# Local attention on one Trainium2 core: probabilities as the stationary operand, v with a ones column as the moving one

## The chip, the cores and the metric

The kernel runs on one core of one Trainium2 chip. The metric is the device time of one execution in microseconds (us), lower being better. Before the change it is 3192.31 us, the median of three runs (3188.84 to 3196.97).

A core has a matrix engine (TensorE, "PE" in the profile, its weight loads listed as "PEld"), a vector engine (VectorE, "DVE"), a scalar engine (ScalarE, "ACT"), a general engine (GpSimd, "POOL") and a queue that issues transfers (SyncE, "SP"). Matrix products land in PSUM, eight banks of 512 float32 values on each of 128 partitions. Everything here is float32.

## The reference

The input is `x`, 8 sequences of 1024 tokens of 256 values. The program first adds a causal latent attention with 16 heads (not touched here), and then a two-layer local transformer. One layer of that is, cut to what matters:

```python
h = shift_token(x)
q, k, v = split(h @ wqkv, 3)            # 8 heads of 64
q, k = rotary_xpos(l2norm(q) * qs, l2norm(k) * ksc)
# windows of 128 queries; each sees its own window and the one before
sim  = einsum('bhwid,bhwjd->bhwij', bq * 8, bk)      # j over 256 keys
mask = (i < j) | (i > j + 128) | (j == -1)
attn = softmax(where(mask, -max, sim))
o    = einsum('bhwij,bhwjd->bhwid', attn, bv)
x = x + o @ wo
x = x + geglu_mlp(layernorm(shift_token(x)))
```

A query `i` of a window sees the keys `j <= i` of its own window and the keys `j >= i` (counted within the window) of the previous one. Of the 128 x 128 square of a query window with its own keys the lower triangle counts, of that with the previous window's keys the upper one.

## The kernel before

The first third of the time is the latent attention. The rest, `local`, works through 128 windows: 2 layers x 8 sequences x 8 windows of 128 tokens. A `Pass` is one layer of one sequence, hence 8 windows `i` = 0 to 7. One loop runs over steps (line 1277), and in each step several windows are at work, each at another stage, so that the engines always have something to do. The order of the instructions on PE, DVE, ACT and POOL is the order in which this loop writes them (`manual_schedule`); the order on SP is not written by hand. In step `s` the loop calls:

- `both` of window `s-4`, then `qk` of window `s` (the product for q and k, norms and rotation), `transposes` of window `s-1`, `v` of window `s`. `transposes` turns q and k in 32 x 32 squares on DVE and then sends them to DRAM and back, which puts the squares into place: four writes of 128 KB and a read of 512 KB on SP.
- an `output` that was put off (see below), a unit of the MLP if one is due, `values` of window `s-4`, and `scores` of window `s-3`.
- the rest of an MLP product if one is pending (`rests`), `divide` of window `s-4`, `output` for the pair of windows `s-6` and `s-5` when `s` is even, and another unit of the MLP. If an MLP product was pending in this step, `output` is put off to the next one (`held`).

`scores` (L999) computes keys x queries: k stationary, q moving, and for each key quarter of 32 only the 160 query columns that can count (fewer in window 7, which has no following window). ACT exponentiates, and POOL sets the masked entries to zero with two `affine_select` per group of four heads. So the probabilities `pts[i][g]` lie with the keys on the partitions; columns 0 to 127 are the queries of the same window, columns 128 to 255 those of the next.

`values` (L1044) makes `v` stationary, 32 columns at a time (L1057), and moves 128 columns of probabilities through it. The four heads of a group write the four 32-partition quarters of the PSUM tile `o`, so four matmuls run side by side. The output is transposed: head dimension on the partitions, queries in the columns, which is what `output` needs as stationary operand. The sums of the exponentials come from a further product with a stationary matrix of ones (L1065) over `both`, for which DVE adds the two squares of probabilities first (L1041). `divide` (L1070) takes the reciprocal of the sums over 128 x 256 values (L1075), multiplies (L1080), and keeps two control sums (L1079, L1084). `output` (L1088) multiplies by `wo` through `times` (L722), which splits the 128 stationary columns into four quarters.

`load_o` (L775) puts the rows of `wo` in the order in which `values` leaves the head dimensions on the partitions. The pools `pacc` (one bank) and `psum` (three banks, tag `mm`) hold `o` and the sums.

Of the kernel before, what the change touches and what calls it, by code (L numbers as in the profile page):

```python
# [29 lines left out]
F32 = mybir.dt.float32  # L30
# [23 lines left out]
LOW, HIGH = 1e-30, 1e10  # L54
# [4 lines left out]
DEPTH, HEADS, DH, WINDOW = 2, 8, 64, 128  # L59
INNER = HEADS * DH  # L60
# [23 lines left out]
def preln_mla_local_kernel(  # L84
# [627 lines left out]
    def local(ctx: ExitStack, verdict):  # L712
# [4 lines left out]
        p1 = ctx.enter_context(tc.tile_pool(name="l1", bufs=1))  # L717
        p2 = ctx.enter_context(tc.tile_pool(name="l2", bufs=2))

        QUARTER = [slice(32 * n, 32 * n + 32) for n in range(4)]  # L720

        def times(out, w, rhs, start, stop):  # L722
            for four in QUARTER:
                nc.tensor.matmul(out[four], w[:, four], rhs, start=start, stop=stop)  # L724

        ppair = [ctx.enter_context(tc.tile_pool(name="pair0", bufs=1, space=PSUM))]
        psum = ctx.enter_context(tc.tile_pool(name="psum3", bufs=3, space=PSUM))
        ppair.append(ctx.enter_context(tc.tile_pool(name="pair1", bufs=1, space=PSUM)))
        pacc = ctx.enter_context(tc.tile_pool(name="pacc3", bufs=1, space=PSUM))
        evac = Evacuate(nc, "a")  # L730

        ones = p1.tile([P, 32], F32, name="ones_l")
        nc.gpsimd.memset(ones, 1.0)
# [53 lines left out]
        def load_mlp(l):  # L787
# [126 lines left out]
        qkT = p1.tile([P, PLACES + 1, 4, 2, 4, 32], F32, name="qkT")  # L914
        zs = [dram.tile([P, 4, 2 * P], F32, tag=f"z{i}", name=f"z{i}") for i in range(4)]
        zxs = [dram.tile([P, 4, 2 * P], F32, tag=f"zx{i}", name=f"zx{i}") for i in range(2)]
        zhs = [dram.tile([P, 4, 2 * P], F32, tag=f"zh{i}", name=f"zh{i}") for i in range(2)]


# [5 lines left out]
        class Pass:  # L925
# [43 lines left out]
            def v(self, i):  # L969
                key = self.key(i)  # L970
                pv = psum.tile([P, INNER], F32, tag="mm", name=f"pv{key}")
                for c in range(2):
                    times(pv, self.left(i)[c], self.w["qkv"][:, c, 2 * INNER :], c == 0, c == 1)
                self.vs[i] = p1.tile([P, INNER], F32, tag="v", name=f"v{key}", bufs=6)
                evac(self.vs[i], pv)

            def transposes(self, i):

# [53 lines left out]
                        )  # L1032
                    self.pts[i].append(pt)

            def both(self, i):

                self.sums = [self.pts[i][g][:, :, :P] for g in range(2)]
                if i:
                    for g in range(2):
                        t = p1.tile([P, 4, P], F32, tag="both", name=f"both{self.key(i)}_{g}", bufs=2)  # L1040
                        nc.vector.tensor_tensor(t, self.sums[g], self.pts[i - 1][g][:, :, P:], ALU.add)  # L1041
                        self.sums[g] = t

            def values(self, i):  # L1044

                key, vs, pts = self.key(i), self.vs, self.pts
                blocks = [(i - 1, P)] if i else []
                blocks.append((i, 0))
                o = pacc.tile([P, 2, 2, P], F32, tag="acc", name=f"o{key}")
                s = psum.tile([P, 2, P], F32, tag="mm", name=f"s{key}")  # L1050
                place = lambda j: 2 * (j % 2) + j // 2
                for g in range(2):
                    for a in range(2):
                        for m, off in blocks:
                            for j in range(4):
                                h = 4 * g + j
                                nc.tensor.matmul(  # L1057
                                    o[32 * j : 32 * j + 32, g, a, :],
                                    vs[m][:, h * DH + a * 32 : h * DH + a * 32 + 32],
                                    pts[m][g][:, place(j), off : off + P],  # L1060
                                    start=(m == blocks[0][0]), stop=(m == i),
                                )
                for g in range(2):
                    for j in range(4):
                        nc.tensor.matmul(  # L1065
                            s[32 * j : 32 * j + 32, g, :], ones, self.sums[g][:, place(j), :], start=True, stop=True
                        )
                self.done[i] = o, s

            def divide(self, i):  # L1070

                key, vs, pts, oTs = self.key(i), self.vs, self.pts, self.oTs
                o, s = self.done.pop(i)
                rs = p1.tile([P, 2, P], F32, tag="lrs", name=f"rs{key}")
                nc.vector.reciprocal(rs, s)  # L1075
                if i % 2 == 0:
                    oTs[i // 2] = p2.tile([P, 4, 2 * P], F32, tag="oT", name=f"oT{key}")
                at = self.n * NT + i
                nc.vector.tensor_reduce(stats[:, 1, at : at + 1], s, AX.XY, ALU.add)  # L1079
                nc.vector.tensor_tensor(  # L1080
                    oTs[i // 2][:, :, (i % 2) * P : (i % 2 + 1) * P].rearrange("p (g a) q -> p g a q", g=2),
                    o, rs.unsqueeze(2).to_broadcast([P, 2, 2, P]), ALU.mult,
                )
                nc.vector.tensor_reduce(stats[:, 0, at : at + 1], rs, AX.XY, ALU.add)  # L1084
                if i:
                    del vs[i - 1], pts[i - 1]

            def output(self, n):  # L1088

                oT = self.oTs.pop(n)  # L1090
                x_, y, key = self.x_, self.y, f"{self.b}_{self.l}"
                two = slice(2 * n, 2 * n + 2)
                ps = psum.tile([P, 2, D], F32, tag="mm", name=f"psw{key}_{n}")
                for i in range(2):
                    for c in range(4):
                        times(ps[:, i, :], oT[:, c, i * P : (i + 1) * P], self.w["o"][:, c, :], c == 0, c == 3)
                nc.vector.tensor_tensor(x_[:, two], ps, x_[:, two], ALU.add)

                rows = slice(2 * n * P, (2 * n + 2) * P)
                nc.sync.dma_start(y[rows, :P].rearrange("(t p) d -> p t d", p=P), x_[:, two, :P])  # L1100
                rows = slice(2 * n * P + 1, (2 * n + 2) * P + 1)
                nc.sync.dma_start(y[rows, P:].rearrange("(t p) d -> p t d", p=P), x_[:, two, P:])
                m, o = divmod(2 * n + 2, ST)
                if o == 0:
                    self.hs[m - 1] = p2.tile([P, ST, D], F32, tag="h", name=f"h{key}_{m - 1}")
                    rows = slice((m - 1) * CH, m * CH)
                    nc.sync.dma_start(self.hs[m - 1], y[rows].rearrange("(t p) d -> p t d", p=P))
# [138 lines left out]
        windows = len(passes) * NT  # L1246
# [29 lines left out]
        with tc.manual_schedule(engines={E.PE, E.DVE, E.Activation, E.Pool}):  # L1276
            for step in range(windows + LAG):
                n, i = divmod(step, NT)
                if step < windows and i == 0:
                    l, b = passes[n]  # L1280
                    if n and b == 0:
                        o = w["o"]
                        w = load_attention(l)
                        w["o"] = o
                    made[n] = Pass(n, l, b, w, *ready.pop(n))
                late = step < windows and n and i == 0 and b == 0
                each(step, "both", 4)
# [5 lines left out]
                while held:  # L1293
                    j = held.pop()
# [33 lines left out]
            for _ in units:  # L1328
                while rests:
                    rests.pop()()  # L1330

        ok = p1.tile([P, 2, B * DEPTH * NT], F32, name="okl")
        for m, top in enumerate((HIGH, 1 / LOW)):
            nc.vector.tensor_scalar(ok[:, m, :], stats[:, m, :], top, None, ALU.is_le)
        verdict.add(ok.rearrange("p m n -> p (m n)"), "local")


    def general_mla(ctx: ExitStack):
# [513 lines left out]
    verdict = Verdict()  # L1852
# [93 lines left out]
```

## Time and profile before

| | |
|---|---|
| median of three runs | 3192.31 us |
| the profiled execution | 3190.63 us, with a span of 3188.9 us |
| granted PE clock in it, as a share | 0.993 |
| `local`, windows of attention and MLP | from about 915 us to the end |

The profile is of a single execution. "Span" is the time from its first to its last instruction. In a row of the costliest groups stand the line, the engine, the operation, what it writes and reads, the shapes and the count; behind the bar the busy time of the group, the mean nanoseconds of one instruction, and the idle time of the engine before it with what ended it. Every float32 matmul of the kernel stands in the trace as two PE records, and as many weight loads. The mean of one PE record is its latency, not what it costs: matmuls overlap, and a length for a whole batch is read from the chain of waits, which lists stretches of the critical path as start, length, engine, tile, line and number of records.

### The profile page before, as it was taken

What the parts mean: (1) busy time and instruction counts of PE and PEld (TensorE: products, weight loads), DVE (VectorE), ACT (ScalarE), POOL (GpSimd) and SP (SyncE); (2) the same over time, 40 slices, a digit from 0 to 9 for tenths busy, and PEclk for the clock granted to TensorE, in tenths of its full rate; (3) what the DMA queues carried; (4) which work ended last, traced back from release to release, by engine and by line L of the source; (5) the groups of instructions that cost most, each with busy time, mean ns of one, the idle gap of its engine ahead of it and who ended that gap; (6) DMA issues with size and microseconds to landing.
All of it is one profiled execution on the core that took longest, in us unless ns stands there. A gap on an engine that the chain in (4) does not pass through costs nothing.

```text
span 3188.9 us, 112507 instructions
## 1 busy us (share of the span) xinstructions
PE 3112.4 (98%) x49986; PEld 1447.9 (45%) x49986; DVE 2619.9 (82%) x3848; ACT 1705.4 (53%) x2114; POOL 1381.7 (43%) x1065
## 2 busy tenths in 40 slices
PE   7999999999878999999999999999999999999998
PEld 2344444444333444445554444454544445444453
DVE  5999999999879878788887878777777877778773
ACT  6888988898722444444444444444444444444441
POOL 1011111110057656565565655555555556555540
PEclk9999999999998999999999999999999999999999
DMA  5333434333334454454544445455545545454431
GB/s 138 76 100 95 104 92 108 96 99 87 108 114 120 106 132 117 125 131 117 135 116 132 116 126 157 124 144 141 144 118 136 132 124 134 137 144 121 121 105 56
DMA packets 411613, 376.98 MB, mean 118 GB/s; under 512 B 174655, under 2 KB 353262, under 8 KB 410990
## 3 DMA queue, kind: packets, MB, share of 16 engines
q1 hardware_dynamic: 409134, 367.29, 43.4%
q8 instruction: 394, 6.46, 0.8%
q10 hardware_dynamic: 1984, 2.41, 0.2%
q14 instruction: 101, 0.83, 0.1%
HBM read 173.82 MB, written 141.00 MB: 99 GB/s over the span
## 4 chain that ended last, share of the span: by engine, by line
PE 67%; DVE 2%; DMA 1%; SPq 1%; POOL 0%; issue 0%; ACT 0%; DVEq 0%; ACTq 0%; POOLq 0%
PE ag L724 19%; PE pair L724 13%; PE psy L724 10%; PE psw L724 7%; PE pv L724 6%; PE o L1057 6%; PE pair L1016 5%; PE s L1065 2%; DMA z<-turned 0%; SPq L904 0%; DMA qkT<-z 0%; DMA zx<-turneds 0%; DVE turned L984 0%; DVE rs L1075 0%; SPq L987 0%
## 5 line engine op out<-in xcount | busy, mean ns | idle before, releaser
L483 DVE TENSOR_TENSOR pt<-pt,er 128x1024 f32<-128x1024 f32 x576 | 676.3, 1220 | 31.9 <-ACT pt L469 26.9
L960 POOL TENSOR_TENSOR t<-t,t 128x1024 f32<-128x1024 f32 x128 | 304.3, 2377 | 803.0 <-DVE t L956 803.0
L724 PE MATMUL ag<-d,l 128*32 128x512 f32 x5632 | 639.7, 593 | 0.9 <-ACT d L1146 0.4
L469 ACT ACTIVATE pt<-sc 128x1024 f32<-128x1024 f32 x576 | 560.2, 1029 | 88.8 <-PE sc L461 72.4
L1022 ACT ACTIVATE pt<-pair 128x1024 f32<-128x1024 f32 (+1 forms) x256 | 235.5, 969 | 538.3 <-PE pair L1016 497.1
L724 PE MATMUL pair<-l_qkv,xT 128*32 128x512 f32 x4096 | 473.6, 598 | 4.1 <-DMA xT<-zx 2.6
L127 POOL TENSOR_TENSOR rn<-ss,half 128x16 f32<-128x16 f32 x128 | 373.0, 2914 | 13.9
L724 PEld LDWEIGHTS ag<-d,l 128*32 128x32 f32 x5632 | 178.5, 110 | 372.6 <-issue 351.6
L423 POOL TENSOR_SCALAR_AFFINE_SELECT er<-er 128x128 f32<-128x128 f32 x64 | 74.3, 1169 | 599.5 <-ACT er L421 598.7
L496 PE MATMUL acc<-pt,v 128*32 128x512 f32 (+3 forms) x3072 | 330.0, 498 | 3.8 <-DVE pt L483 3.5
L951 ACT ACTIVATE sq<-pair 128x1024 f32<-128x1024 f32 x128 | 131.3, 1026 | 348.9 <-issue 308.9
L724 PE MATMUL psy<-l,hid 128*32 128x256 f32 x5120 | 282.1, 379 | 0.0
L724 PEld LDWEIGHTS pair<-l_qkv,xT 128*32 128x32 f32 x4096 | 132.8, 111 | 305.0 <-issue 278.0
L461 PE MATMUL sc<-q,k 32*128 32x512 f32 (+3 forms) x3072 | 248.3, 380 | 13.2 <-DVE x L576 6.9
L953 DVE TENSOR_TENSOR t<-pair,l_cos 128x1024 f32<-128x1024 f32 x128 | 156.0, 1219 | 122.8 <-ACT sq L951 122.5
L966 POOL TENSOR_TENSOR t<-t,rn 128x1024 f32<-128x1024 f32 x128 | 243.5, 1902 | 10.0
L724 PE MATMUL pv<-l_qkv,xT 128*32 128x512 f32 x2048 | 247.1, 592 | 0.0
L1189 DVE SCALAR_TENSOR_TENSOR hid<-ag,l_b,ge 128x512 f32<-128x512 f32 x160 | 116.7, 730 | 158.5 <-ACT ge L1188 87.8
L1057 PEld LDWEIGHTS o<-pt,v 128*32 128x32 f32 x7680 | 215.4, 110 | 67.5 <-issue 51.3
L461 PEld LDWEIGHTS sc<-q,k 32*128 32x128 f32 x3072 | 140.3, 183 | 217.4 <-ACT pt L469 157.4
L1057 PE MATMUL o<-pt,v 128*32 128x128 f32 x7680 | 234.5, 273 | 3.1 <-POOL pt L1024 2.8
L1075 DVE RECIPROCAL rs<-s 128x256 f32<-128x256 f32 x128 | 223.1, 1743 | 15.8 <-PE s L1065 15.7
(266 smaller groups left out, 4532.9 us busy)
## 6 DMA issues: line engine op xcount, KB each, us to landing
z<-turned SPq DMA_DIRECT2D x512, 128.0 KB
qkT<-z SPq DMA_DIRECT2D x128, 512.0 KB
y<-xs SPq DMA_DIRECT2D x128, 128.0 KB
h<-y SPq DMA_DIRECT2D x32, 512.0 KB
zx<-turneds SPq DMA_DIRECT2D x120, 128.0 KB
xT<-zx SPq DMA_DIRECT2D x240, 64.0 KB
zh<-turnedh SPq DMA_DIRECT2D x120, 128.0 KB
d<-zh SPq DMA_DIRECT2D x30, 512.0 KB
```

The costliest lines, as they stand in the source:

```text
L127: nc.gpsimd.tensor_tensor(out_, in_, half[:, :n], ALU.pow)
L461: nc.tensor.matmul(two[n // 2][:, n % 2, lo : lo + w], k[rows], q[rows, h], start=(h == 1), stop=(h == 0),)
L469: nc.scalar.activation(pt, sc, AF.Exp, scale=SCALE)
L483: nc.vector.tensor_tensor(t, t, er.to_broadcast([P, 1024 // w, w]), ALU.mult)
L496: nc.tensor.matmul(self.acc[g][32 * n : 32 * n + 32, q0 - c * 512 :], self.v[:, kb, h * VW - at : h * VW - at + 32], pts[n // 2][:, n % 2, ...
L724: nc.tensor.matmul(out[four], w[:, four], rhs, start=start, stop=stop)
L960: nc.gpsimd.tensor_tensor(t1, t1, t2, ALU.add)
L966: nc.gpsimd.tensor_tensor(t1, t1, rn.unsqueeze(3).to_broadcast([P, 2, HEADS, DH]), ALU.mult)
L1016: nc.tensor.matmul(flat[keys, 2 * j + c, q0:q1].rearrange("p (b t) -> p b t", t=32), qkT[rows, at, t, 1, 2 * g + c, :], q[rows, q0 // 32 : ...
L1022: nc.scalar.activation(pt[:, :, : n * P], flat[:, :, : n * P], AF.Exp, scale=-1.0)
L1057: nc.tensor.matmul(o[32 * j : 32 * j + 32, g, a, :], vs[m][:, h * DH + a * 32 : h * DH + a * 32 + 32], pts[m][g][:, place(j), off : off + ...
L1075: nc.vector.reciprocal(rs, s)
```

## The change

`values` is turned around. The probabilities become the stationary operand, 32 queries at a time, and `v` of one head is the moving operand, with a column of ones behind its 64 columns, so 65 columns. The output then has the queries on the partitions, and column 64 of each head is the sum of its exponentials. `v` is kept in a ring of six tiles whose ones column is written once.

Of the two squares of each head, the parts that the mask leaves empty are partly left out. Queries 0 to 63 see only keys 0 to 63 of their own window, and queries 64 to 127 see only keys 64 to 127 of the previous one. So for each head and query quarter there are one matmul over all 128 keys and one over 64 keys. First come all the matmuls over 128 keys, then all those over 64; the column quarters and the two PSUM banks are arranged so that consecutive matmuls fall on different parts of the array. In window 0 of a pass, which has no previous window, one of the two matmuls falls away.

`divide` takes two small reciprocals, multiplies twice, and then transposes the 128 x 512 result in 32 x 32 squares on DVE. After every odd window the pair goes to DRAM in four transfers and comes back in one, as q and k do. `output` uses this as the stationary operand. `both`, the ones matrix, the product of sums and the two control sums fall away; the control sums are replaced by a check of the kept reciprocals every 32 windows. `wo` is loaded in its natural order with one transfer.

```diff
-        ones = p1.tile([P, 32], F32, name="ones_l")
-        stats = p1.tile([P, 2, B * DEPTH * NT], F32, name="stats")
+        LOOK = 32
+        stats = p1.tile([P, LOOK, 2, 4], F32, name="stats")
+        VL = DH + 1
+        vring = [p1.tile([P, HEADS, VL], F32, name=f"lv{i}") for i in range(6)]
+        for t in vring:
+            nc.gpsimd.memset(t[:, :, DH:], 1.0)
...
         def load_o(l):
-            for g in range(2):
-                for j in range(4):
-                    h = 4 * g + j
-                    nc.sync.dma_start(
-                        w[32 * j : 32 * j + 32, 2 * g : 2 * g + 2],
-                        wo[l, h * DH : (h + 1) * DH].rearrange("(a p) e -> p a e", a=2),
-                    )
+            nc.sync.dma_start(w, wo[l].rearrange("(c p) e -> p c e", p=P))
...
-                evac(self.vs[i], pv)
+                self.vs[i] = vring[(self.n * NT + i) % len(vring)]
+                evac(self.vs[i][:, :, :DH], pv.rearrange("p (h d) -> p h d", d=DH))
...
-            def both(self, i):
...
+            def values(self, i):
+                banks = [
+                    pool.tile([P, 512], F32, tag=tag, name=f"o{key}_{r}")
+                    for r, (pool, tag) in enumerate(((pacc, "acc"), (psum, "mm")))
+                ]
+                o = [t[:, : 4 * VL].rearrange("p (h d) -> p h d", d=VL) for t in banks]
+                place = lambda j: 2 * (j % 2) + j // 2
+                todo = []
+                for h in range(HEADS):
+                    todo += [(h, s, i - 1 if s < 2 else i, slice(0, P)) for s in range(4)]
+                for n in range(4):
+                    for r in range(2):
+                        h = 4 * (n // 2) + 2 * r + n % 2
+                        todo += [
+                            (h, s, *((i, slice(0, 64)) if s < 2 else (i - 1, slice(64, P)))) for s in range(4)
+                        ]
+                todo = [(h, s, m, rows, (h // 2 % 2, (s + h // 2 * 2) % 4)) for h, s, m, rows in todo if m >= 0]
+                first, last = ({at: n for n, (*_, at) in every} for every in (
+                    reversed(list(enumerate(todo))), enumerate(todo)
+                ))
+                for n, (h, s, m, rows, (r, c)) in enumerate(todo):
+                    g, j = divmod(h, 4)
+                    q0 = 32 * s + (P if m < i else 0)
+                    nc.tensor.matmul(
+                        o[r][32 * c : 32 * c + 32, 2 * g + h % 2, :], self.pts[m][g][rows, place(j), q0 : q0 + 32],
+                        self.vs[m][rows, h, :], start=first[r, c] == n, stop=last[r, c] == n,
+                    )
+                self.done[i] = o
+
+            def divide(self, i):
+                o = self.done.pop(i)
+                on = p1.tile([P, INNER], F32, tag="on", name=f"on{key}")
+                for r in range(2):
+                    rs = stats[:, (self.n * NT + i) % LOOK, r]
+                    nc.vector.reciprocal(rs, o[r][:, :, DH])
+                    nc.vector.tensor_tensor(
+                        on.rearrange("p (g r j d) -> p r g j d", g=2, r=2, j=2)[:, r],
+                        o[r][:, :, :DH].rearrange("p (g j) d -> p g j d", g=2),
+                        rs.rearrange("p (g j) -> p g j", g=2).unsqueeze(3).to_broadcast([P, 2, 2, DH]), ALU.mult,
+                    )
+                if i % 2 == 0:
+                    self.ot = p1.tile([P, 4, 2, 4, 32], F32, tag="ot", name=f"ot{key}")
+                nc.vector.transpose(self.ot[:, :, i % 2], on.rearrange("p (y x d) -> p x y d", y=4, x=4))
+                if i % 2:
+                    z = zos[i // 2 % 2]
+                    for c in range(4):
+                        nc.sync.dma_start(
+                            z.rearrange("(x p) c f -> p x c f", p=32)[:, :, c],
+                            self.ot[32 * c : 32 * c + 32].rearrange("p x i y t -> p x (i y t)"),
+                        )
+                    oTs[i // 2] = p2.tile([P, 4, 2, 4, 32], F32, tag="oT", name=f"oT{key}")
+                    nc.sync.dma_start(
+                        oTs[i // 2].rearrange("p c i y t -> p (c i y t)"), z.rearrange("p c f -> p (c f)")
+                    )
...
             def output(self, n):
-                        times(ps[:, i, :], oT[:, c, i * P : (i + 1) * P], self.w["o"][:, c, :], c == 0, c == 3)
+                        for s, four in enumerate(QUARTER):
+                            nc.tensor.matmul(
+                                ps[four, i, :], oT[:, (s + 2 * c) % 4, i, c, :], self.w["o"][:, c, :],
+                                start=c == 0, stop=c == 3,
+                            )
...
-                each(step, "both", 4)
...
+                if step >= 4 and (step - 3) % LOOK == 0 and step - 4 < windows:
+                    inverses = stats.rearrange("p n r h -> p (n r h)")
+                    ok = p1.tile([P, INNER], F32, tag="on", name=f"okl{step}")[:, : LOOK * HEADS]
+                    nc.vector.tensor_scalar(ok, inverses, 1 / LOW, None, ALU.is_le)
+                    nc.vector.scalar_tensor_tensor(ok, inverses, 1 / HIGH, ok, ALU.is_ge, ALU.mult)
+                    verdict.add(ok, "local")
```

More of the change, by code (lines that the diff above doesn't have):

```diff
@@ L730, in local @@
         evac = Evacuate(nc, "a")
-        ones = p1.tile([P, 32], F32, name="ones_l")
-        nc.gpsimd.memset(ones, 1.0)
         rest_hid = p1.tile([P, CH // 2], F32, name="rest_hid")
@@ L916, in local @@
         zxs = [dram.tile([P, 4, 2 * P], F32, tag=f"zx{i}", name=f"zx{i}") for i in range(2)]
+        zos = [dram.tile([P, 4, 2 * P], F32, tag=f"zo{i}", name=f"zo{i}") for i in range(2)]
         zhs = [dram.tile([P, 4, 2 * P], F32, tag=f"zh{i}", name=f"zh{i}") for i in range(2)]
@@ L973, in v @@
                     times(pv, self.left(i)[c], self.w["qkv"][:, c, 2 * INNER :], c == 0, c == 1)
-                self.vs[i] = p1.tile([P, INNER], F32, tag="v", name=f"v{key}", bufs=6)
-                evac(self.vs[i], pv)
+                self.vs[i] = vring[(self.n * NT + i) % len(vring)]
+                evac(self.vs[i][:, :, :DH], pv.rearrange("p (h d) -> p h d", d=DH))
             def transposes(self, i):
@@ L1033, in scores @@
                     self.pts[i].append(pt)
-            def both(self, i):
-                self.sums = [self.pts[i][g][:, :, :P] for g in range(2)]
-                if i:
[L1039 to L1086, printed above, removed]
+            def values(self, i):
+                key = self.key(i)
+                banks = [
[25 more added lines that the diff above has]
+                self.done[i] = o
@@ new lines, in divide @@
+            def divide(self, i):
+                key, oTs = self.key(i), self.oTs
+                o = self.done.pop(i)
[22 more added lines that the diff above has]
+                    )
+                if i:
+                    del self.vs[i - 1], self.pts[i - 1]
@@ L1330, in local @@
                     rests.pop()()
[L1332 to L1335, printed above, removed]
     def general_mla(ctx: ExitStack):
```

## The prediction

> **What bounds the kernel now.** I read the engine totals first, then the stretch in which the windows run steadily (1250 to 3100 us), then the chain of waits.
>
> ```profile
> PE 3112.4 (98%) x49986; PEld 1447.9 (45%) x49986; DVE 2619.9 (82%) x3848; ACT 1705.4 (53%) x2114; POOL 1381.7 (43%) x1065
> 1250.00:3100.00 1850.00, 1845.87 (x33132) 906.57 (x33128) 1472.67 (x2324) 807.55 (x956) 1036.87 (x767) 1.00 0.49 130
> ```
>
> The second line gives the busy time of PE, weight loads, DVE, ACT and POOL in these 1850 us, then the PE clock (full), the DMA share and GB/s. PE is idle for 4.1 us of 1850, DVE for 377. A busy PE need not be a fast one, so I ask whether its batches last as long as their columns take. Three rows by shape and seven pieces of the chain of waits:
>
> ```profile
> L1057 PE MATMUL o<-pt,v 128*32 128x128 f32 x7680 | 234.5, 273 | 3.1 <-POOL pt L1024 2.8 <-DVE oT L1080 0.2
> L1016 PE MATMUL pair<-qkT 64*32 64x160 f32 x7168 | 152.2, 304 | 19.2 <-DMA qkT<-z 16.0 <-DVE t L956 2.8 <-issue 0.5
> L1016 PE MATMUL pair<-qkT 64*32 64x32 f32 x256 | 14.3, 200 | 0.6 <-issue 0.6
> ...
> 2022.13 1.75 PE o L1057 x64
> 2023.87 0.44 PE s L1065 x16
> 2024.31 1.25 PE pair L1016 x64
> ...
> 2037.73 0.87 PE o L1057 x32
> ...
> 2040.29 3.59 PE psw L724 x64
> ...
> 2078.39 0.86 PE psy L724 x32
> ...
> 3109.42 1.04 PE pair L1016 x30
> ```
>
> From 160 to 32 columns a record gets 104 ns shorter, 0.81 ns a column; I use 0.833, with which the batches come out. Four records run side by side on the four column quarters: 64 records of 128 columns are 64 x 128 x 0.833 / 4 = 1.71 us, and the chain has 1.75, which is 0.7 ns more per record. With 64 rows, two halves of the rows work at once as well: the rest of psy, 32 records of 256 columns over eight parts, is 0.85 us by this sum and 0.86 in the chain. So PE time is columns moved, divided by the parts that work at once, and what shortens this stream shortens the kernel.
>
> **PE: the values.** Removed per window: 1.75 (L1057) + 0.44 (L1065) = 2.19 us; in the 16 first windows of a pass, 0.87 + 0.44 = 1.31.
>
> Added: 32 matmuls of 128 keys, 64 records of 65 columns over four parts: 64 x (65 x 0.833 / 4 + 0.7) = 0.91 us. Then 32 of 64 keys, 64 records over eight parts: 0.43 us by columns. Here records would start every 7 ns, and the question is whether PE can be fed so fast. The nearest row is the last piece above, the scores of window 7 (its list is short because the rest of psy starts among them; by line it has 64 records). Its longest column quarter, 128 columns, sets the stream at 0.85 us, and it takes 1.04, a record every 16 ns; the excess of 0.19 is that of the other scores (1.25 against 1.07). In the trace the first 16 records of a scores batch start within 133 ns, and later, where nothing was queued, new matmuls (two records each) come 16.7 ns apart. That feed, 8.35 ns a record, makes 0.53 us; with some matmuls queued from the slower part before, I take 0.50. Sum 1.41 us, 0.78 saved, x 112 = 87 us. Bounds: 0.43 without any limit at the feed, against 16 ns a record throughout, which gives 2.09 and saves 0.10.
>
> First windows: 32 records over 128 keys and 32 over 64, the latter only on the lower rows, so four parts each: 0.90 us, 0.41 saved, x 16 = 7 us. **Together -94 us.**
>
> [...]
>
> psw (L724) keeps 64 records of 256 columns. The v copy on ACT (0.59 us) writes runs of 64: zero, behind 44% busy.
>
> **DVE.** Removed per window, from the rows: reciprocal 1.74, control sums 0.36 + 0.41, product 0.67, both 1.36. Added: two reciprocals of 4 columns (nearest: 0.24 us for 16), two products of 128 x 256 (0.42 each, from L551), a transpose like L984 (0.68): 2.0. That is 2.5 us less, over 300 us in all, but hidden behind PE: 4 us of PE waits are left in the steady stretch. It pays in the ramp, where DVE is busy 94.5 of the 105 us from 945 to 1050 and PE idle for 17.4. I take -6, bounds 0 and -12.
>
> **The transfers: the added wait.** psw now waits for a round trip through DRAM. It is built like the one for q and k:
>
> ```profile
> 2021.34 1.80 SPq L987 DMA_DIRECT2D z<-turned  x4
> 2026.37 0.34 SPq L991 DMA_DIRECT2D qkT<-z  x1
> ...
> 3136.84 0.36 SPq L1107 DMA_DIRECT2D h<-y  x1
> ...
> 3140.71 0.43 DVE L837 BATCH_NORM_STATS2 bnsth<-h 128x6 f32<-128x256 f32 x1 [1.25 <-DMA h<-y]
> ```
>
> From the first of four writes to the read 5.0 us; from a 512 KB read to its first reader 3.9. With `divide` at 2.0 and up to 1.7 before DVE takes it up, oT is there 11 to 13 us after the last product of the odd window. From the trace, the old psw starts 15.9 us or more after it in nearly all pairs (2024.3 to 2040.3 in the lines above; 26 where `output` is held); a shorter stream takes about 0.8 of that. So 2 to 4 us are left. Behind the waiting psw on PE stand all later matmuls, so any lateness counts in full. Two exceptions: at the end the slack is 6.6 us (last sums end 3121.4, psw starts 3128.1), which costs about 5 us, and the third-last pair has 11.6, about 1. The first pairs have 17 to 18, inside the ramp. Cost: +6, nothing at best. On SP the five issues per pair take some 2 us, and the read blocks it for some 3 while the writes land; behind it stand xs, y and the next z, whose readers come a step later or more. 64 pairs of 0.5 MB out and back add 64 MB to 377: the DMA share rises from 0.49 towards 0.58. `load_o` with one transfer for eight, and the check every 32 windows (three small DVE operations): zero.
>
> The second PSUM bank is now taken at the third head, 1.5 us earlier than the sums took it. Its previous reader can be L1097, which 2.5 us less DVE work per step moves forward. Zero.
>
> **Sum.** -94 - 6 + 6 = -94 on the execution's own 3190.6: 3096.6. The median of the runs lies 1.7 higher: **3098 us**, own range 3065 (0.43 us, full relief in the ramp, no stall) to 3130.
>
> **Rivals.** *The row halves don't work side by side.* Then the second part takes 0.91 us too, a window saves 0.37: 41 + 7 = 48, hence 3144. Against it: psy's rest. [...] *PE can't be fed.* At 16 ns a record the sum is 11 + 16 x 0.27 = 16 us saved: 3176. For it: no batch of 64 in the trace goes below 16 ns. Against it: that batch is as long as its longest quarter. *oT comes late (slower).* The place is psw in every second pair, 32 of 64, where `output` isn't held. If SP sends the new transfers behind others, or landing takes longer at the higher DMA share, so that the round trip needs 19 us instead of 12, each of the 32 loses 4 us: +128 - 94 = +34, 3226. It decides from a trip of 18 us, where 32 x 2.9 eats the gain. For it: SP waits 658 us in total at L987, up to 18.6 at once, and what is put behind that waits along. Against it: in the old order the next L987 comes some 12 us after `divide`, and the writes of y go out promptly.
>
> **Chances.** Forecast 0.55, halves in turn 0.10, feed 0.15, late oT 0.20. A measurement can tell 0.3%, some 9.6 us. The first two are faster, the third faster with 0.09 and the same with 0.06, the last slower: 0.74, 0.06, 0.20. The range leaves out most of the last case and runs from 3065 to 3205.
>
> **What would show it.** The chain should have about 1.4 us of o before each scores batch, no s, scores unchanged; DVE busy near 2300; PE before psw idle for under 10 us. If o takes 2 us, the feed or the halves are the answer (the two parts stand apart by rows, 128 and 64); if psw waits for oT by microseconds in every second pair, the last rival. Equal PE time per window and yet no gain would prove me wrong about the bound.

## The result, and the profile after the change

The changed kernel takes 3289.99 us (median of four runs, 3281.02 to 3299.19), the kernel before it on the same chip 3190.57. The ratio is 1.0309, with an interval of 1.0275 to 1.0343: some 99 us slower, where 94 us less were forecast. The profiled execution, the fastest of the four, took 3281.02 us, with a span of 3279.3 and a mean PE clock of 0.986.

From the page of the kernel after: the engine totals, the queue that brings the program to the engines (packets, MB, share), and three groups of instructions.

```profile
PE 3084.3 (94%) x55618; PEld 1436.9 (44%) x55618; DVE 2361.4 (72%) x3761; ACT 1708.1 (52%) x2114; POOL 1373.4 (42%) x1070
...
q8 instruction: 438, 7.18, 0.9%
...
L1109 PE MATMUL psw<-l_o,oT 128*32 128x256 f32 x4096 | 252.4, 396 | 33.4 <-DMA oT<-zo 23.1
...
L1014 PE MATMUL pair<-qkT 64*32 64x160 f32 x8192 | 196.2, 297 | 90.4 <-issue 64.9
...
L982 DVE STREAM_TRANSPOSE turned<-t 128x512 f32<-128x512 f32 x256 | 166.0, 685 | 126.6 <-DMA zh<-turnedh 65.5
```

And its steady stretch, by engine as before the prediction:

```profile
1250.00:3100.00 1850.00, 1765.94 (x36624) 868.42 (x36617) 1228.06 (x2193) 782.33 (x923) 1007.64 (x745) 1.00 0.56 156
```

PE did get less work, but now it stands idle: 84 of 1850 us, where it had been 4. DVE does less, as forecast, and also stands still more. What PE waits for (us in all, times, longest):

```profile
PE pair L1014 <- issue: 64.9, 40, 3.5
PE pair L1014 <- DMA qkT<-z: 25.0, 6, 9.6
PE psw L1109 <- DMA oT<-zo: 23.1, 10, 8.0
...
PE psw L1109 <- issue: 9.7, 5, 6.4
```

The new wait for oT is there, but the largest item is one that no data explains: 40 times PE stops inside a batch of scores, up to 3.5 us, and waits for nothing that the profile shows ("issue"). The same view of the kernel before has two such stops, of 1.0 us in all:

```profile
PE pair L1016 <- issue: 1.0, 2, 0.6
```

The chain of waits of the changed kernel shows both (o is the values, pair in L1014 the scores, psw the output product, and ag and psy are the MLP):

```profile
2000.47 3.99 DMA oT<-zo
2004.46 0.14 issue
2004.60 5.40 PE psw L1109 x64
...
2027.16 1.71 PE o L1064 x117
2028.87 1.15 PE pair L1014 x64
...
2045.66 1.64 PE o L1064 x113
2047.30 0.03 PE pair L1014 x2
2047.34 0.03 PE o L1064 x2
2047.37 0.89 PE pair L1014 x29
2048.26 1.76 issue
2050.02 0.19 PE pair L1014
...
2056.41 3.45 PE psw L1109 x64
```

From 2027.16 the step runs as it was meant to: 2.86 us for values and scores, where the old kernel took 3.44. From 2045.66 it doesn't: after 29 score records PE stops for 1.76 us and then goes on with the scores. At 2004.60 there is a second surprise: an output product that takes 5.40 us instead of 3.45, after a long wait.

A total by stage comes from the trace, as the time from a window's first product with v to the first matmul of what follows its scores (so it also holds the wait of a psw that follows), summed over the windows but the last:

| kernel | median window | sum |
|---|---|---|
| before | 3.54 us | 456.0 us |
| after | 3.34 us | 505.8 us |
| e1 (doubled, no new transfers) | 3.78 us | 530.9 us |
| e2 (after, without transfers) | 2.98 us | 462.6 us |
| e3 (wide) | 2.96 us | 429.7 us |
| e4 (wide, without transfers) | 2.96 us | 386.3 us |

This stage was to lose 94 us, and gained 50.

### The profile page after: what moved, and what is told of

Its sections match the earlier page's. It is cut to its first block, busy times and chain, and to the rows that moved or that the text cites. A ratio compares the mean times of both kernels' runs of the same rounds, so it can differ in the third digit from the quotient of the medians.

```text
span 3279.3 us, 124228 instructions
## 1 busy us (share of the span) xinstructions
PE 3084.3 (94%) x55618; PEld 1436.9 (44%) x55618; DVE 2361.4 (72%) x3761; ACT 1708.1 (52%) x2114; POOL 1373.4 (42%) x1070
## 4 chain that ended last, share of the span: by engine, by line
PE 83%; DMA 7%; issue 3%; DVE 3%; SPq 3%; ACT 1%; POOL 1%; ACTq 0%; DVEq 0%; POOLq 0%
PE ag L724 17%; PE pair L724 12%; PE psy L724 9%; PE acc L496 8%; PE psw L1109 7%; PE sc L461 6%; PE pv L724 5%; PE o L1064 5%; PE pair L1014 4%; PE psR L202 2%; PE psq L202 2%; DMA zo<-ot 2%; PE psx L202 1%; DMA oT<-zo 1%; SPq L901 1%
## 5 line engine op out<-in xcount | busy, mean ns | idle before, releaser
L724 PE MATMUL ag<-d,l 128*32 128x512 f32 x5632 | 657.5, 595 | 4.8 <-ACT pt L1020 2.3
L724 PE MATMUL pair<-l_qkv,xT 128*32 128x512 f32 x4096 | 480.4, 595 | 4.9 <-issue 2.2
L724 PEld LDWEIGHTS ag<-d,l 128*32 128x32 f32 x5632 | 193.6, 110 | 372.2 <-issue 344.6
L1109 PE MATMUL psw<-l_o,oT 128*32 128x256 f32 x4096 | 252.4, 396 | 33.4 <-DMA oT<-zo 23.1
L1014 PE MATMUL pair<-qkT 64*32 64x160 f32 x8192 | 196.2, 297 | 90.4 <-issue 64.9
L724 PEld LDWEIGHTS pair<-l_qkv,xT 128*32 128x32 f32 x4096 | 140.4, 110 | 298.6 <-issue 271.7
L1064 PEld LDWEIGHTS o<-lv,pt 128*32 128x32 f32 (+1 forms) x15360 | 222.1, 108 | 82.6 <-issue 59.9
L982 DVE STREAM_TRANSPOSE turned<-t 128x512 f32<-128x512 f32 x256 | 166.0, 685 | 126.6 <-DMA zh<-turnedh 65.5
L724 PE MATMUL pv<-l_qkv,xT 128*32 128x512 f32 x2048 | 256.5, 592 | 0.0
L1064 PE MATMUL o<-lv,pt 128*32 128x65 f32 (+1 forms) x15360 | 241.9, 222 | 7.3 <-issue 4.4
```

Of the source, the lines that this page charges most:

```text
L982: nc.vector.transpose(t[:, :, n], r[:, n])
L1014: nc.tensor.matmul(flat[keys, 2 * j + c, q0:q1].rearrange("p (b t) -> p b t", t=32), qkT[rows, at, t, 1, 2 * g + c, :], q[rows, q0 // 32 : ...
L1064: nc.tensor.matmul(o[r][32 * c : 32 * c + 32, 2 * g + h % 2, :], self.pts[m][g][rows, place(j), q0 : q0 + 32], self.vs[m][rows, h, :], sta ...
L1109: nc.tensor.matmul(ps[four, i, :], oT[:, (s + 2 * c) % 4, i, c, :], self.w["o"][:, c, :], start=c == 0, stop=c == 3,)
```

## The experiments

Theory: PE can't get its *program* fast enough in the new burst. The rival: the round trip of oT through DRAM, with its waits and its traffic, is what costs. Ratios are to the kernel before, run on the same chip. The runs stand on several chips, on which the kernel before takes 3189 to 3197 us; so runs of different chips are compared below by their ratios, 0.1% being 3.2 us.

| run | median us | ratio, 95% interval |
|---|---|---|
| e1_split_moving | 3286.82 | 1.0298, 1.0278 to 1.0318 |
| e2_no_trip | 3226.78 | 1.0099, 1.0082 to 1.0115 |
| e3_wide | 3204.38 | 1.0031, 1.0019 to 1.0044 |
| e4_wide_no_trip | 3141.88 | 0.9837, 0.9821 to 0.9853 |
| e5_wide_hold | 3322.6 | 1.0425, 1.0405 to 1.0445 |
| e6_even_split | 3198.46 | 1.0030, 1.0018 to 1.0042 |
| e7_trip_unread | 3168.56 | 0.9935, 0.992 to 0.995 |
| e8_hold_lag13 | 3231.45 | 1.0115, 1.0098 to 1.0132 |
| e9_hold_lag12 | 3262.2 | 1.0206, 1.0186 to 1.0226 |
| e10_trip_on_pool | 3198.95 | 1.0008, 0.9994 to 1.0022 |
| e11_trip_on_act | 3411.4 | 1.0675, 1.0653 to 1.0697 |
| e12_ends_on_pe | 3206.85 | 1.0033, 1.0021 to 1.0045 |
| e13_by_window | 3242.55 | 1.0138, 1.0121 to 1.0155 |

### e1: the old kernel with twice as many value matmuls of half the length

```diff
+                        for half in (0, 64):
...
-                                    o[32 * j : 32 * j + 32, g, a, :],
+                                        o[32 * j : 32 * j + 32, g, a, half : half + 64],
...
-                                    pts[m][g][:, place(j), off : off + P],
+                                        pts[m][g][:, place(j), off + half : off + half + 64],
```

> The kernel before, with each product of values and probabilities cut into two of 64 columns: 64 matmuls a window instead of 32, the same columns, no new transfer. Theory 'loading of instructions' (PE runs dry because its program is loaded in pieces of 16 KB and the batch from the values to the scores now uses them up faster than they come): the batch grows from 72 to 104 matmuls, more than the changed kernel has (96), so PE halts of 1 to 3 us, ended some 1.4 us after a packet of the instruction queue, appear in many windows: +30 to +100 us, 3220 to 3290. Theory 'transfers' (the added round trip through DRAM delays PE, or the heavier DMA traffic delays everything that is loaded): nothing is added to the traffic, so 3190 to 3205.

The old kernel became 2.98% slower, nearly as slow as the changed one, with no new transfer, no new order and as many columns. Its PE waits, first line:

```profile
PE pair L1016 <- issue: 45.5, 45, 3.5
```

The same stops, in the same place. Its typical window grew by 0.24 us (about 30 us in all); the stops make most of the rest of the 91.

### e2, e3, e4: without the transfers, with half as many value matmuls, with both

e2 feeds the output from what the transpose leaves on the chip:

```diff
-                    self.ot = p1.tile([P, 4, 2, 4, 32], F32, tag="ot", name=f"ot{key}")
+                    self.ot = p2.tile([P, 4, 2, 4, 32], F32, tag="oT", name=f"ot{key}")
...
-                    z = zos[i // 2 % 2]
-                    for c in range(4):
-                        nc.sync.dma_start(
...
+                    oTs[i // 2] = self.ot
```

e3 makes the stationary side 64 queries wide instead of 32, so that a window has 32 value matmuls instead of 64, for the same columns and the same result:

```diff
-                    todo += [(h, s, i - 1 if s < 2 else i, slice(0, P)) for s in range(4)]
+                    todo += [(h, s, i - 1 if s < 2 else i, slice(0, P)) for s in (0, 2)]
...
-                            (h, s, *((i, slice(0, 64)) if s < 2 else (i - 1, slice(64, P)))) for s in range(4)
+                            (h, s, *((i, slice(0, 64)) if s < 2 else (i - 1, slice(64, P)))) for s in (0, 2)
...
-                        o[r][32 * c : 32 * c + 32, 2 * g + h % 2, :], self.pts[m][g][rows, place(j), q0 : q0 + 32],
+                        o[r][32 * c : 32 * c + 64, 2 * g + h % 2, :], self.pts[m][g][rows, place(j), q0 : q0 + 64],
```

e4 is both edits together.

> The changed kernel without the four writes and the read of each pair; the output product reads the transposed tile as it lies, so its terms are in the wrong places. Left out is that regrouping alone. Theory 'loading of instructions': the halts inside the values and scores stay (about 85 us in the steady stretch), and only the waits of the output product for its tile, the slower ramp and the slow clock after long waits go, some 30 to 50 us: 3235 to 3265. Theory 'transfers': all of the loss goes and the saved PE time shows: 3110 to 3140.

> The changed kernel with 64 instead of 32 queries stationary in each product of the values: 32 matmuls a window instead of 64, the same columns in time, transfers unchanged. Theory 'loading of instructions': the batch from values to scores has 64 matmuls, fewer than before the change (72), the halts fall from about 90 us to under 15: 3170 to 3210 if the weight loads of 64 columns stay hidden, up to 3290 if each adds its own time[...]. Theory 'transfers': traffic and waits are the same, 3275 to 3300.

> Both edits, 64 queries stationary and no round trip (the regrouping of the outputs left out). If the two causes add up and nothing else is at work, the saved PE time of 0.5 to 0.8 us a window shows: 3090 to 3130. If it stays above 3180, a third cause is left that neither theory has.

The two causes add up. By the ratios, leaving the transfers out saves 67 us, and 62 when done to the wide form. Halving the value matmuls saves 89, and 84 without the transfers. Neither is the whole. e2 keeps the stops; in e3 they are gone:

```profile
PE pair L1014 <- issue: 52.2, 35, 3.8
```

```profile
PE psw L1109 <- DMA oT<-zo: 39.1, 14, 8.1
PE pair L1014 <- DMA qkT<-z: 22.0, 6, 9.9
```

The first fence is from e2's PE waits, the second holds the first two lines of e3's: what leads there now is oT. Without transfers and with the wide form, the steady stretch of e4 is as full as the old one, PE 1845 of 1850 us, and the kernel some 50 us faster than before (without the regrouping, so it is no replacement):

```profile
1250.00:3100.00 1850.00, 1845.46 (x32074) 865.59 (x32068) 1275.81 (x2294) 812.60 (x965) 1026.72 (x765) 1.00 0.48 131
```

### e6: as many more matmuls, but spread out

e1 could also mean that more matmuls cost by themselves. e6 adds to the old kernel exactly as many as the change (2816), but in the first MLP product, whose matmuls are long:

```diff
-                    for c in range(2):
-                        times(
-                            ps.rearrange("p (s a t) -> p s a t", a=4, t=32), w["1"][:, c, i, :], d[:, c],
-                            c == 0, c == 1,
-                        )
+                    for s in range(2):
+                        for c in range(2):
+                            times(
+                                ps.rearrange("p (s a t) -> p s a t", a=4, t=32)[:, 2 * s : 2 * s + 2],
+                                w["1"][:, c, i, :], d[:, c, 2 * s : 2 * s + 2], c == 0, c == 1,
+                            )
```

> The kernel before, with the first products of the MLP cut into two of 256 columns each: 2816 matmuls more, as many as the change added, but where PE needs 107 ns for each, so a piece of 16 KB lasts 6.9 us and not under 2. If the halts come from the rate at which instructions are used up in the batch, no halt is added: 3190 to 3210. If they come from the number of instructions loaded (so many pieces, so much lost at each), the loss is that of e1_split_moving: 3260 to 3290.

It costs 0.3%, and "issue" in its scores is 1.6 us. So the number isn't it; the density in the burst is. The queue that brings the program says how. Its line on the page of the kernel before:

```profile
q8 instruction: 394, 6.46, 0.8%
```

A packet is 16 KB (6.46 MB / 394). The change adds 44 packets for 2816 matmuls, e6 the same 44; e1 has 454 for 3840 more than before, e3 378 for 1024 fewer. All four give 64 matmuls to a packet. A packet takes about 1 us to come (median 1.00 in the changed kernel, a tenth of them over 1.38). Between the start of a window's values and the end of its scores, the old kernel consumes 72 matmuls in 3.54 us, the new one 96 in 2.98: a packet lasts 3.1 us before, 2.0 after, 2.3 in e1 (104 in 3.78) and 3.0 in e3 (64 in 2.96). The stop at 2048.26 in the chain, seen in the transfers of the half microsecond from 2047.0 on:

```profile
q8 instruction: 1, 0.02, 17.3%
```

One packet starts there and takes 17.3% of 16 x 0.5 us, 1.38 us. It lands between 2048.4 and 2048.9, and PE resumes at 2050.02. All 13 stops that I followed in this way, from 2403 to 2910 us, end 1.2 to 1.6 us after such a landing. Counting from 1050 to 3100 us each stretch between two PE starts that exceeds the columns moved by over 0.15 us and ends 1.1 to 1.75 us after a landing, the stops make 85.3 us in the changed kernel, 60.8 in e1, 80.7 in e2, 3.3 in e3, 4.0 in e6, and 2.9 before.

The place of the stops says the same. Number PE's matmuls in the order of their starts. In the changed kernel 59 stretches between 1050 and 3100 us exceed the columns moved by over 0.6 us. Of these, 55 end within 1.5 matmuls of the border of a piece: whole multiples of 64 apart, less a steady drift of 0.23 of a matmul a piece, which by my estimate is room for about one instruction of another kind, since a matmul has four records in the trace, two of PE and two weight loads (the first border and the drift are fitted to the stops themselves). The other four are three waits for oT and a gap in ag. In e1 all 49 such stretches end at borders; by chance it would be one in twenty. Three stops in a row, from the chain of the changed kernel, with 191.5 matmuls from each to the next, three pieces less half a matmul:

```profile
2601.87 0.91 issue
2602.78 0.48 PE pair L1014 x9
...
2620.95 0.86 issue
2621.80 0.69 PE pair L1014 x15
...
2638.16 1.76 issue
2639.92 0.76 PE pair L1014 x27
```

That the arrival of the program is the cause rests on these borders, on the landings and on the three runs that vary density and number apart (e1, e3, e6); the profile has no row that names it. How far ahead a piece is asked for, and so why a stop lasts as long as it does, stays open.

### e7: the round trip made, but read by nobody

To split the 62 us of the transfers, e7 is e3 with all transfers made, while the output reads what is on the chip:

```diff
-                    self.ot = p1.tile([P, 4, 2, 4, 32], F32, tag="ot", name=f"ot{key}")
+                    self.ot = p2.tile([P, 4, 2, 4, 32], F32, tag="ot", name=f"ot{key}")
...
-                    oTs[i // 2] = p2.tile([P, 4, 2, 4, 32], F32, tag="oT", name=f"oT{key}")
+                    back = p1.tile([P, 4, 2, 4, 32], F32, tag="oT", name=f"oT{key}")
...
-                        oTs[i // 2].rearrange("p c i y t -> p (c i y t)"), z.rearrange("p c f -> p (c f)")
+                        back.rearrange("p c i y t -> p (c i y t)"), z.rearrange("p c f -> p (c f)")
...
+                    oTs[i // 2] = self.ot
```

> 64 queries stationary, all five transfers of a pair made, but the output product reads the transposed tile as it lies (the regrouping left out), so that nobody waits for them. Against e3_wide (3204) and e4_wide_no_trip (3142): if the loss is waiting alone, 3142 to 3155; if the traffic or the queue order costs by itself, 3180 to 3204.

3168.6: by the ratios some 31 us of the 62 are the wait for oT, and 31 are the transfers' presence in itself. The largest change that goes with the presence is in the DVE waits, of e4 and then of e7:

```profile
DVE turned L982 <- DMA zx<-turneds: 11.7, 9, 5.2
...
DVE turned L982 <- DMA zh<-turnedh: 3.0, 7, 0.7
```

```profile
DVE turned L982 <- DMA zh<-turnedh: 67.2, 24, 5.2
DVE turned L982 <- DMA zx<-turneds: 61.0, 18, 9.9
```

The tag `turned` has one buffer, which the transposes of q and k share with those of the rows sent to zx and zh for the next products. DVE may write it again only when the writes that read it have left the SP queue and landed, and these now stand behind five more transfers per pair. DVE isn't what bounds the kernel, though; of its 128 us only a part reaches PE, which waits longer for qkT than in e4 (27.6 us against 12.7) and for hid:

```profile
PE pair L1014 <- DMA qkT<-z: 27.6, 7, 9.5
PE ag L724 <- DVE hid L1206: 12.4, 7, 3.0
```

A second buffer of `turned` wasn't tried, so this path is argued and not shown; e10 below speaks against its being the whole.

### e5, e8, e9: the output product a step later

The chain says that oT is late, so give it another step. e5 puts off every output of e3 to the next step; e8 (shown) and e9 (12) also start the MLP units two steps and one step later:

```diff
-        LAG = 11
+        LAG = 13
...
-                    if full and step + 1 < windows:
+                    if step + 1 < windows:
```

> 64 queries stationary, and the output product of every pair put off to the next step (before: only of every second one), which gives the round trip about 6 us more. If the cost of the round trip is the waiting of the output product, most of the 62 us between e3_wide and e4_wide_no_trip come back: 3145 to 3170, below the kernel before. If it is the traffic, or the order of the queue, which delays the other transfers too, little comes back: 3190 to 3205.

> e5_wide_hold with the MLP two steps later (LAG 13 instead of 11). In e5_wide_hold the lines of h arrived too late for the statistics of the next MLP chunk, and VectorE stood in front of them for 266 us, since the put-off pair is the one that completes a chunk. If that is all that was wrong there, the two steps remove it, the round trip has its 6 us more, and what is left is the cost of the traffic seen in e7_trip_unread and two steps more at the end (some 10 us): 3160 to 3190, perhaps just below the kernel before. If holding the product back costs by its place (PSUM banks, DVE order), it stays above 3250.

> The same with one step later (LAG 12). The MLP's rest then falls in odd steps, so fewer things meet in one step; h has one step more. Same two readings: 3160 to 3195 if the late h was the cause, above 3250 if the place of the product is.

All are slower than e3. In e5, the MLP's input is complete only with the put-off pair, and DVE stands in front of it:

```profile
DVE bnsth L834 <- DMA h<-y: 266.1, 30, 10.9
```

By the ratios, moving the MLP recovers 99 (two steps) and 70 us (one step) of the 126 lost, and not the rest: in e9 PE waits 39.2 us at its values for DVE's use of the output product (L1113), in e8 29.2 us for qkT. No order tried had room for a later output.

### e10, e11: the transfers on another queue

e10 is e3 with the five transfers of a pair on POOL's queue, e11 the same with `nc.scalar`:

```diff
-                        nc.sync.dma_start(
+                        nc.gpsimd.dma_start(
...
-                    nc.sync.dma_start(
+                    nc.gpsimd.dma_start(
```

> 64 queries stationary, and the five transfers of a pair issued by GpSimd instead of SP, so that they neither wait behind other transfers nor hold them up. GpSimd has about 9 us idle in each step, but stands in front of its own waits. If the loss is the order on SP's queue: 3150 to 3185. If it is the length of the round trip and the traffic, whichever queue: 3195 to 3215. If GpSimd, standing before a landing, comes late to the masks or rotations: above 3215.

> The same with ScalarE issuing the five transfers. ScalarE has more room (44% busy) but feeds PE's next products sooner. Order on SP's queue as the cause: 3150 to 3185; length and traffic: 3195 to 3215; ScalarE late to the gelu, the exponentials or the copies: above 3215.

On POOL's queue the kernel equals the one before (1.0008), some 7 us better than e3, with psw still waiting 26.3 us for oT. DVE's waits in front of `turned` fall from 133 us in e3 to 43, and the time hardly follows. So of the readings given beforehand, the length of the round trip and the traffic fits, and the order of SP's queue doesn't. The test isn't a clean one, since POOL itself now stands in front of the landing of its writes:

```profile
POOL oT L1094 <- DMA zo<-ot: 234.4, 63, 7.0
```

On ACT's queue the kernel loses 206 us against e3: an issue there that waits for a landing holds up what stands behind it, here the MLP's activations. From ACT's waits in e11:

```profile
ACT L1214 <- DMA zo<-ot: 268.0, 30, 11.4
...
ACT L1204 <- DMA zo<-ot: 150.2, 18, 10.5
```

### e12, e13: no round trip at the ends; a round trip for each window

In e12 the first six windows and the last two of the whole run are transposed by PE, four transposes each and a copy by ACT, the others as in e3. e13 is e12 with the round trip for each window instead of each pair, so ten transfers a pair.

```diff
+                near = self.n == 0 and i < 6 or self.n == len(passes) - 1 and i >= 6
+                if near:
...
+                    for y in range(4):
+                        nc.tensor.transpose(
+                            ps[:, y].rearrange("p x t -> p (x t)"), on[:, y * P : (y + 1) * P], ident
+                        )
+                    evac(oTs[i // 2][:, :, i % 2].rearrange("p x y t -> p y x t"), ps)
+                else:
```

> 64 queries stationary; in the first six windows of the first pass and the last two of the last one, PE transposes the output (four more matmuls and an ACT copy a window) in place of the round trip. If the waits at the ends cost what the stretches say, 12 us in the ramp and 9 at the end, less some 2 for the transposes: 3204 - 15 to 20, 3180 to 3192, at or just below the kernel before. If the ramp is bound by other transfers anyway: 3198 to 3206.

> e12_ends_on_pe with a round trip for each window instead of each pair: the same bytes, ten transfers a pair instead of five; the even window's half is sent one step earlier, and the output product can start on it. If waiting is what costs in the steady stretch (about 25 us in e3_wide's trace): 15 to 25 us below e12_ends_on_pe, 3160 to 3175, below the kernel before. If traffic and the number of transfers cost: no faster than e12_ends_on_pe, or slower by up to 20 us.

e12 gains nothing over e3. Its first eight windows take 127.2 us against 130.9 in e3's trace, 4 us gained of the 12 expected. Its waits say why: the ramp now waits for DVE's reciprocals in front of the transposes.

```profile
PE pso L1089 <- DVE stats L1077: 26.3, 8, 4.6
PE psw L1120 <- DMA oT<-zo: 22.7, 10, 4.3
```

In e13 no wait of PE for oT is left among the large ones (0.9 us), and the kernel is 36 us slower than e12: DVE comes late. Its waits in front of `turned` are no longer than in e12 (121 us against 132); new is the one for h, and PE waits for DVE in turn:

```profile
DVE bnsth L834 <- DMA h<-y: 73.0, 15, 6.2
```

```profile
PE psy L724 <- DVE on L1078: 25.9, 13, 2.7
```

So here the number of transfers costs by itself, at equal bytes: ten a pair instead of five, 36 us. Not all of this was foreseen: e1, e3, e6, e10 and e11 fell in a range given beforehand and e9 in that of its second reading, while e2 came out 8 us below its nearer range, e12 1 us above, e7 and e8 between theirs, and e4, e5 and e13 slower than the ranges of their readings. No version tried with the whole computation is faster than the kernel before; e10 ties with it.

## Why the prediction was wrong

**The bound: right.** PE set the pace, and e4 shows that its shorter stream pays: with PE fed and the transfers gone, the kernel is some 50 us faster, for a stage that is 70 us shorter (386.3 against 456.0). Part of the difference is known by place only: in the windows 8 to 119 of e4's trace, values and scores are 60 us shorter and the MLP's products, ag and psy, 16 us longer than before. Why stays open.

**PE's columns: right for the array.** The part over 128 keys starts a group of four records every 57 ns and takes 0.91 us as worked out from the columns; the weight loads beside them, 110 ns a record in the mean, add nothing to that. Nor does any run show the 0.8 us a window that e3's expectation allowed for weight loads of 64 columns: its window takes 2.96 us, e2's with 32 columns 2.98. The halves work side by side: the first 32 records over 64 keys start within 0.27 us, 8.4 ns each, so the first rival falls. After that new matmuls come 16.7 ns apart, so that the second part takes 0.66 us instead of 0.50; the scores too begin more slowly, their first 16 records within 0.30 us (median) where the old kernel has 0.21. So a window without a stop takes 2.98 us instead of 3.54: 0.57 saved, not 0.78. Over 112 windows that is 64 us instead of 87.

**The step that failed** is "the question is whether PE can be fed so fast". I answered it with the gap between two matmuls in a short batch, and took the worst case to be 16 ns a record, which still saves time. The feed has a second limit that doesn't show in a gap: the program itself arrives in pieces of 64 matmuls, and the burst here, which uses one up in 2.0 us, ran into stops of up to 3.5 us that ended 1.2 to 1.6 us after a piece had landed. My bounds thus ended at a small gain where a loss of 94 us was possible (85.3 in the steady stretch, 8.9 in the tail). The rival "PE can't be fed" named the place, with the wrong mechanism and the wrong sign. e1 shows that limit with no transfer added: 91 us for nothing but more and shorter matmuls in the burst.

**The transfers: a term mis-sized**, +6 where e2 measures +67. The wait isn't in every second pair, as the rival "oT comes late" had it, but in 10 of 64, with 23.1 us, half of it in the ramp; with stops elsewhere PE is late itself, and without them (e3) it is 14 waits and 39.1 us. I had costed the queue behind the new transfers at nothing ("whose readers come a step later or more"): e7 puts what the transfers cost without a reader at 31 us. By what path is not shown: e10 takes them off SP's queue and gains only 7. And a late psw costs more than the wait: after a wait it took 5.40 us instead of 3.45, begun at a clock of 0.50 (below). The tail from window 120 on grew from 174.3 to 191.5 us, where I had 5 or 6; the last psw waits for oT to 3214.99 and then takes 6.06 us, with the clock at 0.50 from 3215 to 3218.

**DVE's relief in the ramp: wrong sign.** The first eight windows take 131.7 us instead of 118.3, for -6 forecast. Without the transfers the wide form takes 113.7 (e4), so the relief exists, and the wait for oT covers it.

The rest of my signs held: DVE busy 2361 for "near 2300" (258 us less, where I had worked out over 300), no s, oT's moves within the DMA share that I gave (0.56 for 0.58).

In sum, 193 us lie between forecast and result. By the ratios, 89 are the density of the value matmuls (changed kernel to e3), 56 the transfers beyond my 6 (e3 to e4), and 48 that e4 gains 52 where 100 were forecast without transfers; the slower feed makes 23 of these 48. By place, the two traced executions differ by 90.4 us: 1.8 before the first window, 13.4 in the first eight, 58.0 in windows 8 to 119 and 17.3 in the tail.

## What to carry to other kernels

Before splitting matmuls into more and shorter ones, count how many the densest stretch consumes per microsecond and compare that with how the program arrives: here 64 in 3 us ran through, 64 in 2.3 or in 2 us stopped. A mean over the whole kernel says nothing of it; the same 2816 matmuls spread out cost 0.3%. And a round trip through DRAM isn't priced by its own latency alone: made but read by nobody, it still cost half of its 62 us.

## What the hardware showed beyond that

After the waits below the PE clock was lower, 0.50 and then 0.87 of full, so that they cost more than their own length. In the stretches around 2000 us in the changed kernel PE waits 5.75 us for qkT, until 1999.36, and 2.84 us for oT, until 2004.60 (last figures: PE clock, DMA share, GB/s):

```profile
1996.00:2004.50 8.50, 2.39 (x64) 1.59 (x64) 0.55 (x2) 3.33 (x3) 2.40 (x4) 0.61 0.76 241
2004.50:2007.50 3.00, 2.90 (x28) 1.57 (x32) 2.10 (x5) 0.00 (x0) 0.00 (x0) 0.50 1.01 357
2007.50:2010.00 2.50, 2.50 (x44) 1.52 (x40) 1.57 (x4) 0.00 (x0) 0.00 (x0) 0.87 0.65 104
2010.00:2016.00 6.00, 6.00 (x60) 1.88 (x56) 3.13 (x4) 0.69 (x1) 0.00 (x0) 1.00 0.72 163
```

The clock stands at 0.50 for 3 us after PE has work again, and at 1.00 from 2010 on. The psw that waited took 5.40 us instead of 3.45, 1.95 us on top of the waits.
